# Attention probabilities turned in 32 x 32 blocks on VectorE and rearranged through DRAM

## The chip, the cores and the metric

The kernel runs on one core of a Trainium2 chip. The metric is the time of one execution on the device, in microseconds (us). The engines of the core run their own instruction streams in program order and wait for each other by semaphores: TensorE (PE in the profile, its weight loads are PEld), VectorE (DVE), ScalarE (ACT), GpSimd (POOL) and SyncE (SP, which issues transfers). ScalarE and GpSimd can issue transfers too.

## The reference

One pre-norm decoder layer in float32 on 4 sequences of 512 tokens with 512 channels: gated linear attention, cross attention to 256 context tokens with quantized probabilities, and a block of causal attention with a mixture of experts. The change lies in the causal attention: 16 heads of 128 channels in 4 groups that share keys and values, cut here to its core.

```python
def causal_attention(x1, h):                 # one sequence, S = 512
    q, k = rope(rmsnorm(h @ wq)), rope(rmsnorm(h @ wk))
    v = h @ wv
    q, k, v = heads(q, 16), heads(k, 4), heads(v, 4)     # 128 channels each
    for head in range(16):
        s = q[head] @ k[head // 4].T / sqrt(128)
        p = softmax(where(causal, s, -inf))              # (queries, keys)
        o[head] = p @ v[head // 4]
    return x1 + concat(o) @ wo
```

TensorE sums over the partitions of both its operands. The probabilities come out with queries on partitions, and `p @ v` sums over keys, so each block of 128 x 128 of `p` must be brought to keys on partitions first.

## The kernel before

The 2048 tokens are worked in 16 blocks of 128 (number `i`, with `c = i % 4` the place in its sequence). Block `i` sees `c + 1` blocks of keys. Its attention runs over four groups `g` of four heads; the four heads of one group in one block are called a set here, 64 sets in all.

For a set, `scores` multiplies on TensorE (line 1333), masks the diagonal and finds the maxima on VectorE (1335 to 1337), exponentiates on ScalarE (1339) into four tiles `e[0]` to `e[3]`, one a head with 128 queries on partitions, and divides by the sums on VectorE (1341, 1343). `values` then turns each 128 x 128 block on TensorE against the identity (1364), four heads into one PSUM tile, copies that tile to SBUF on ScalarE (1366, tile `eT`, three buffers) and multiplies the 512 columns by the values' weights (1360, 1370) into the PSUM tile `po`, which VectorE copies to `oT` (1372). `project` multiplies by the output weights (1380).

`attention` runs these one set apart: `scores` of set g + 1, then `project` of g - 1, then `values` of g. The tiles of `e` come in two lots of four (`xa`, and `og` with `x_in`), so one set is scored while the other is used.

The functions are Python generators. `weave` interleaves several streams of them: the attention of block `i` at virtual time `i`, the projections `qkv` of a later block, cross attention (`crossing`, with `norms`), `rest_of` and others. Each `yield` is one step; the dictionary `steps` (lines 152, 153) says how many steps a generator is thought to have, and so how its steps are spread; after a first run of a kind the count found takes its place. The order so made is the program order of every engine.

PSUM tiles of the name `pb` come from a pool of six buffers, for all streams. Weights are loaded in pieces of 512 KB by SP (`load_q`, line 1230, four buffers; `load_o`, line 1239, three), each issued behind the matmul that freed its buffer. SP also stores and reloads activations through DRAM (271, 274, 279, 355, 1197, 1401, 1425, 1434, 1436). In cross attention SP stores the quantized queries (271) and reads them back in four transfers (279) that wait for that store.

At the end of the stage `load_experts` loads the expert weights (1690 to 1694) while the last block's attention runs; then the experts follow (`turned`, `gate_up`, `down`).

Of the kernel before, what the change touches and what calls it, by code (L numbers as in the profile page):

```python
# [31 lines left out]
F32 = mybir.dt.float32  # L32
BF16 = mybir.dt.bfloat16
AF = mybir.ActivationFunctionType
ALU = mybir.AluOpType
# [4 lines left out]
P = 128  # L40
B, S, D = 4, 512, 512
NT = B * S // P
TB = S // P
KD = D // P
# [60 lines left out]
def decoder(ctx: ExitStack, tc: tile.TileContext, a: dict, out: bass.AP):  # L105
    nc = tc.nc
# [6 lines left out]
    ident = tab[:, C_ID, :]  # L113
# [36 lines left out]
            yield from g  # L150

    steps = {"first_o": 3, "cross": 37, "qkv": 12, "rest_of": 5, "route": 10, "enter": 8, "spares": 24, "load": 26}
    steps.update((f"attention{c}", n) for c, n in enumerate((37, 41, 53, 57)))

    def weave(*streams):

# [46 lines left out]
    dram = ctx.enter_context(tc.tile_pool(name="dram", bufs=1, space=DRAM))  # L203
# [6 lines left out]
    def transposed(src, pool, name, bufs=2):  # L210

        kind, eye = (F32, ident) if src.dtype == F32 else (BF16, ident_i)
        tp = p_b.tile([P, KD, P], kind, name="pb")
        for kd in range(KD):
            nc.tensor.transpose(tp[:, kd, :], src[:, kd * P : (kd + 1) * P], eye)
        t = pool.tile([P, KD, P], kind, name=name, bufs=bufs)
        nc.scalar.copy(t, tp)
        return t
# [23 lines left out]
    hTs, x2s, xis, fronts = {}, {}, {}, {}  # L242
# [135 lines left out]
    with ExitStack() as st:  # L378
# [18 lines left out]
        p_b = st.enter_context(tc.tile_pool(name="a_pb", bufs=4, space=PSUM))  # L397
# [674 lines left out]
        start = prologue(0)  # L1072
# [69 lines left out]
    with ExitStack() as st:  # L1142
        keep = st.enter_context(tc.tile_pool(name="b_keep", bufs=1, reuse_waits="tile"))
        small = st.enter_context(tc.tile_pool(name="b_small", bufs=4, reuse_waits="tile"))
        p_b = st.enter_context(tc.tile_pool(name="b_pb", bufs=6, space=PSUM, reuse_waits="tile"))
# [3 lines left out]
        wa = st.enter_context(tc.tile_pool(name="b_a", bufs=2, reuse_waits="tile"))  # L1149
        mid = st.enter_context(ExitStack())  # L1150
        wq_ = mid.enter_context(tc.tile_pool(name="b_q", bufs=2, reuse_waits="tile"))
# [39 lines left out]
        def norms(i):  # L1191


            x2 = x2s.pop(i)
            x3 = wq_.tile([P, D], F32, name="x3", bufs=1)
            yield from layernorm(x3.unsqueeze(1), x2.unsqueeze(1), small)
            nc.sync.dma_start(x3d[i], x3)
            h = wq_.tile([P, D], F32, name="h3", bufs=1)
            ss = small.tile([P, 1], F32, name="rms_s")
            nc.scalar.activation(h, x3, AF.Square, accum_out=ss)  # L1200
            yield
            r = small.tile([P, 1], F32, name="rms_r")
            rsqrt(r, ss, small, add=1e-6, mul=1.0 / D)
            yield
            nc.vector.tensor_scalar(h, x3, r, None, ALU.mult)
            yield
            tp = p_b.tile([P, KD, P], F32, name="pb")
            hTs[i] = wq_.tile([P, KD, P], F32, name="hT", bufs=2)
            for kd in range(KD):
                nc.tensor.transpose(tp[:, kd, :], h[:, kd * P : (kd + 1) * P], ident)  # L1210
            for kd in range(KD):
                nc.scalar.activation(hTs[i][:, kd, :], tp[:, kd, :], AF.Identity, scale=ln1[:, kd : kd + 1])
            yield
# [35 lines left out]
                load_o()  # L1249
                yield  # L1250

        zero = wa.tile([P, 4, P], F32, name="eT", bufs=3).rearrange("p a b -> p (a b)")
        nc.gpsimd.memset(zero, 0.0)
        nc.gpsimd.dma_start(hd[CAP : CAP + P], zero)
        nc.gpsimd.dma_start(spares[0 : 2 * NE * P].rearrange("(p n) c -> p (n c)", p=P), zero[:, 0 : 4 * NE])
# [60 lines left out]
        def scores(i, g, out):  # L1316

            c = i % TB
            at = (i - c) % RING
            runs = [(0, at, min(c + 1, RING - at))]  # L1320
            if at + c + 1 > RING:
                runs.append((RING - at, 0, at + c + 1 - RING))
            nk = (c + 1) * P
            qT, rq = qs[i]
            both = 2 if c < 2 else 1
            e = [ao.tile([P, S], F32, name="xa", bufs=4) for _ in range(4)] if g % 2 == 0 else [ao.tile([P, S], F32, name=n, bufs=2) for n in ("og", "og", "x_in", "x_in")]
            es = small.tile([P, 4], F32, name="es")
            nm = small.tile([P, 4], F32, name="nm")
            for n in range(0, 4, both):
                ps = p_b.tile([P, both, S // both], F32, name="pb")  # L1330
                for m in range(both):
                    for k, j, w in runs:
                        nc.tensor.matmul(ps[:, m, k * P : (k + w) * P], qT[g][:, n + m, :], kT[:, g, j : j + w, :], start=True, stop=True)  # L1333
                diag = ps[:, :, nk - P : nk]
                nc.vector.tensor_tensor(diag, diag, over(tab[:, C_CAUSAL, :], both), ALU.add)
                nc.vector.tensor_reduce(nm[:, n : n + both], ps[:, :, :nk], AX.X, ALU.max, negate=True)
                nc.vector.tensor_scalar(nm[:, n : n + both], nm[:, n : n + both], rq, None, ALU.mult)
                for m in range(both):
                    nc.scalar.activation(e[n + m][:, :nk], ps[:, m, :nk], AF.Exp, bias=nm[:, n + m : n + m + 1], scale=rq, accum_out=es[:, n + m : n + m + 1])  # L1339
                yield  # L1340
            nc.vector.reciprocal(es, es)
            for n in range(4):
                nc.vector.tensor_scalar(e[n][:, :nk], e[n][:, :nk], es[:, n : n + 1], None, ALU.mult)
            out.append(e)
            yield

        def attention(i):


            c = i % TB  # L1350
            vals = [kv[k] for k in range(i - c, i + 1)]
            oTs = []

            def values(g, e):
                po = p_1.tile([P, 4, P], F32, name="po")
                eTs = []
                for k in range(c + 2):
                    if k > c:
                        yield
                        nc.tensor.matmul(po, vals[c][:, g, :], eTs[c], start=c == 0, stop=True)  # L1360
                        break
                    tp = p_b.tile([P, 4, P], F32, name="pb")
                    for n in range(4):
                        nc.tensor.transpose(tp[:, n, :], e[n][:, k * P : (k + 1) * P], ident)  # L1364
                    eT = wa.tile([P, 4, P], F32, name="eT", bufs=3)
                    nc.scalar.copy(eT, tp)  # L1366
                    eTs.append(eT)
                    yield
                    if k:
                        nc.tensor.matmul(po, vals[k - 1][:, g, :], eTs[k - 1], start=k == 1, stop=False)  # L1370
                oTs.append(wa.tile([P, 4, P], F32, name="oT"))
                nc.vector.tensor_copy(oTs[-1], po)  # L1372
                yield

            def project(g):
                oT = oTs.pop(0)
                for h in range(0, 4, 2):
                    w = ahead_o.pop(0)
                    for m in range(2):
                        nc.tensor.matmul(pw, oT[:, h + m, :], w[:, m, :], start=g == 0 and h + m == 0, stop=g == 3 and h + m == 3)  # L1380
                    load_o()
                    yield

            es = early.pop(i, [])
            if not es:
                yield from scores(i, 0, es)
            for g in range(4):
                if g < 3:
                    yield from scores(i, g + 1, es)
                elif i + 1 < NT:  # L1390
                    while i + 1 not in qs:
                        yield
                    early[i + 1] = []
                    yield from scores(i + 1, 0, early[i + 1])
                if g == 1:
                    pw = p_1.tile([P, D], F32, name="pw")
                if g > 0:
                    yield from project(g - 1)
                if g == 3:
                    x3 = wa.tile([P, D], F32, name="x3_in")  # L1400
                    nc.sync.dma_start(x3, x3d[i])
                yield from values(g, es.pop(0))
            del qs[i]
            yield
            yield from project(3)
            nc.vector.tensor_tensor(x3, pw, x3, ALU.add)
            xs[i] = x3
# [13 lines left out]
        def rest_of(i):  # L1421

            x1 = xs.pop(i)
            x2 = ao.tile([P, D], F32, name="acc", bufs=1)
# [10 lines left out]
            nc.gpsimd.tensor_tensor(x2, x2, x1, ALU.add)  # L1435
            stored.append(nc.sync.dma_start(out[i * P : (i + 1) * P], x2).ins.name)
            yield
            hT = transposed(h, wa, "eT", bufs=3)
            yield

            parts = p_b.tile([P, P], F32, name="pb")
# [275 lines left out]
        for i in range(NT - 1):  # L1717
            g, kind = rest_of(i), "rest_of"
# [49 lines left out]
        def turned(b):  # L1768
            t = rows_of.pop(b)
            tp = p_b.tile([P, KD, P], F32, name="pb")  # L1770
            for kd in range(KD):
                nc.tensor.transpose(tp[:, kd, :], t[:, kd, :], ident)
            hTs[b] = wa.tile([P, KD, P], F32, name="eT", bufs=3)
            nc.vector.tensor_copy(hTs[b], tp)

        def gate_up(b):
# [128 lines left out]
```

## Time and profile before

| | |
|---|---|
| time, median of 3 runs | 3330.07 us (3327.7 to 3330.5) |
| the profiled execution's own time, and its span | 3329.88 us, 3328.1 us |
| attention stage (first score block to line 1406 of the last) | about 1951 to 3096 us |
| in it: PE, DVE, ACT, POOL busy | 1119, 706, 592, 228 us |
| transfers from 1950 to 3100 us | 216 MB, SP's hardware queue 56.7% of the 16 DMA engines' time |

The profile lists, for one execution, busy time by engine, groups of instructions by source line, and the order of time. Matmuls are pipelined, so the price of one is the distance between starts and not its listed duration; a float32 matmul is listed as two passes. A float32 transpose is one pass of 128 columns. Issues of transfers on SP and ScalarE are listed as SPq and ACTq and don't count as busy.

### The profile page before, as it was taken

The page shows a single profiled execution, that of the slowest core. Times are in us where ns is not written, and L with a number is a line of the kernel's source. Part 1 is how long each engine was busy: PE and PEld are TensorE (multiplying, and loading weights), DVE is VectorE, ACT ScalarE, POOL GpSimd, SP SyncE. Part 2 cuts the span into 40 slices and gives each one's busy share as a digit, 9 for nine tenths or more (in the row PEclk, how much of TensorE's full clock was granted, in tenths as well). Part 3 has the DMA queues.
Part 4 walks back from the last instruction along what each step waited for, and adds up shares of the span by engine and source line. Part 5 has one row for each costly group of instructions (what it writes and reads, how often), then busy time and mean ns, then how long its engine had stood idle before and what let it go on. Part 6 is the DMA issues. An engine that isn't in the chain of part 4 may idle for free. (4 is left out here: it accounts for less than half of the span.)

```text
span 3328.1 us, 48186 instructions
## 1 busy us (share of the span) xinstructions
PE 3166.4 (95%) x16015; PEld 1775.2 (53%) x16015; DVE 1831.9 (55%) x4184; ACT 1606.6 (48%) x4391; POOL 1465.7 (44%) x2780
## 2 busy tenths in 40 slices
PE   5899999999999999999998789999999999999998
PEld 3555555555555555555555445555555555555444
DVE  5665555546555556555454566656665665646211
ACT  3445555545554455545453346455555555645222
POOL 1156757676666666676765211112212221121443
PEclk8999999999999999999998799999999999999999
DMA  6343534444444434454434455556655565567454
GB/s 171 103 134 114 145 103 131 138 124 126 118 129 137 133 117 121 124 148 126 121 108 120 144 178 185 176 161 186 183 167 165 184 168 155 175 198 263 93 89 60
DMA packets 491032, 476.09 MB, mean 143 GB/s; under 512 B 225332, under 2 KB 340554, under 8 KB 490656
## 3 DMA queue, kind: packets, MB, share of 16 engines
q1 hardware_dynamic: 477616, 444.59, 45.5%
q0 software_dynamic: 11728, 25.58, 3.8%
q8 instruction: 128, 2.10, 0.3%
q10 hardware_dynamic: 1440, 2.84, 0.3%
q14 instruction: 120, 0.98, 0.1%
HBM read 411.23 MB, written 61.69 MB: 142 GB/s over the span
## 5 line engine op out<-in xcount | busy, mean ns | idle before, releaser
L598 PE MATMUL pb<-xnT,w 128*128 128x512 f32 x2048 | 958.6, 603 | 0.5 <-DVE at L674 0.2
L598 PEld LDWEIGHTS pb<-xnT,w 128*128 128x128 f32 x2048 | 364.8, 192 | 340.4 <-issue 333.5
L609 DVE SCALAR_TENSOR_TENSOR cv<-pb,pp,cv 128x510 f32<-128x510 f32 (+2 forms) x576 | 424.3, 746 | 92.7 <-ACT cv L606 79.4
L752 POOL TENSOR_TENSOR iT<-iT,iW 64x126 f32<-64x126 f32 (+22 forms) x930 | 344.7, 371 | 72.8
L1267 PE MATMUL pb<-c_q,hT 128*128 128x512 f32 x768 | 353.0, 599 | 3.3 <-DMA c_q<-in_c_wq_dram 1.6
L751 POOL TENSOR_TENSOR iW<-iA,iT 64x126 f32<-64x126 f32 (+22 forms) x930 | 321.6, 346 | 65.7 <-issue 0.2
L1186 POOL TENSOR_TENSOR rope_s<-q,tab 128x128 f32<-128x128 f32 x80 | 45.0, 563 | 481.6 <-DVE q L1297 368.3
L972 PE MATMUL pb<-wot,og 128*128 128x512 f32 x512 | 247.6, 607 | 5.5 <-DVE xa L977 4.5
L1267 PEld LDWEIGHTS pb<-c_q,hT 128*128 128x128 f32 x768 | 141.4, 192 | 157.4 <-issue 147.3
L606 ACT ACTIVATE cv<-pb,pp 128x512 f32<-128x512 f32 x192 | 148.7, 774 | 148.1 <-PE pb L598 144.2
L653 POOL TENSOR_TENSOR rk<-ss,mhalf 128x8 f32<-128x8 f32 x32 | 77.7, 2428 | 276.3 <-DVE ss L652 276.3
L977 DVE TENSOR_TENSOR xa<-pb,xa 128x512 f32<-128x512 f32 x112 | 77.1, 688 | 187.2 <-PE pb L972 187.2
L306 ACT ACTIVATE x_e<-pb,nm,x_step 128x256 f32<-128x256 f32 x256 | 141.2, 565 | 57.8 <-DVE nm L302 56.7
L1380 PE MATMUL pw<-wot,oT 128*128 128x512 f32 x344 | 162.6, 599 | 1.6 <-DVE oT L1372 1.3
L1333 PE MATMUL pb<-kT,qT 128*128 128x256 f32 (+3 forms) x576 | 163.2, 409 | 0.8 <-ACT og L1339 0.7
L705 POOL TENSOR_TENSOR qg<-qh,row 128x512 f32<-128x512 f32 x64 | 82.8, 1293 | 171.7 <-ACT qh L612 149.2
L972 PEld LDWEIGHTS pb<-wot,og 128*128 128x128 f32 x512 | 92.6, 192 | 100.2 <-issue 89.2
L612 ACT ACTIVATE qh<-cv 128x512 f32<-128x512 f32 x64 | 40.4, 631 | 212.8 <-DVE cv L609 212.8
L1782 PE MATMUL pb<-w_gu,eT 128*128 x288 | 130.3, 595 | 3.1 <-issue 3.1
L1366 ACT COPY eT<-pb 128x512 f32<-128x512 f32 x160 | 91.5, 596 | 85.2 <-PE pb L1364 84.3
L132 POOL TENSOR_TENSOR rms_r<-rsq,mhalf 128x1 f32<-128x1 f32 x48 | 27.3, 570 | 220.4 <-DVE rsq L131 220.4
L458 ACT ACTIVATE em<-em,ee 128x128 f32<-128x128 f32 x256 | 78.3, 388 | 94.5 <-POOL ee L655 81.6
(436 smaller groups left out, 6239.9 us busy)
## 6 DMA issues: line engine op xcount, KB each, us to landing
c_q<-in_c_wq_dram SPq DMA_DIRECT2D x128, 512.0 KB
w<-in_a_w_dram SPq DMA_DIRECT2D x124, 512.0 KB
wot<-in_c_wo_dram SPq DMA_DIRECT2D x86, 512.0 KB
row<-g_d SPq DMA_DIRECT2D x64, 512.0 KB
c_o<-in_c_wo_dram SPq DMA_DIRECT2D x42, 512.0 KB
at_d<-at SPq DMA_DIRECT2D x64, 256.0 KB
rrow<-r_d SPq DMA_DIRECT2D x32, 512.0 KB
T<-t_d SPq DMA_DIRECT2D x32, 512.0 KB
```

The source lines that it names most:

```text
L306: nc.scalar.activation(e[:, 2 * r + g, :], ps[r][:, g, :], AF.Exp, bias=nm[:, r, g : g + 1], scale=step[:, h : h + 1], accum_out=ssum[:, g ...
L598: nc.tensor.matmul(pj, wt[:, kd, p * P : (p + 1) * P], xnT[:, kd, :], start=kd == 0, stop=kd == KD - 1)
L606: nc.scalar.activation(ac, pj, AF.Identity, bias=cb[:, m, h : h + 1], scale=cw[:, m, h, 3:4])
L609: nc.vector.scalar_tensor_tensor(ac[:, j:], pj[:, : S - j], cw[:, m, h, 3 - j : 4 - j], ac[:, j:], ALU.mult, ALU.add)
L751: eng.tensor_tensor(u, A[:, i, i + 1 :].unsqueeze(2).to_broadcast([nb, n, w]), T[:, i, :w].unsqueeze(1).to_broadcast([nb, n, w]), ALU.mult)
L752: eng.tensor_tensor(T[:, i + 1 :, :w], T[:, i + 1 :, :w], u, ALU.add)
L972: nc.tensor.matmul(pw, og[p][:, c * P : (c + 1) * P], wot[:, p, :], start=p == 0, stop=p == HG - 1)
L1267: nc.tensor.matmul(pj, hT[:, kd, :], w[:, kd % 2, :], start=kd == 0, stop=kd == KD - 1)
L1333: nc.tensor.matmul(ps[:, m, k * P : (k + w) * P], qT[g][:, n + m, :], kT[:, g, j : j + w, :], start=True, stop=True)
L1366: nc.scalar.copy(eT, tp)
L1380: nc.tensor.matmul(pw, oT[:, h + m, :], w[:, m, :], start=g == 0 and h + m == 0, stop=g == 3 and h + m == 3)
L1782: nc.tensor.matmul(pg, hT[:, kd, :], w_gu[:, bass.ds(e, 1), kd, :, :], start=kd == 0, stop=kd == KD - 1)
```

## The change

The transposes on TensorE, their PSUM tiles and the copies on ScalarE go. In their place, at the end of `scores`:

1. VectorE turns each head's probabilities in blocks of 32 x 32 (four instructions a set, 128 x 128(c + 1) each), into one tile `t` with one buffer. Within each quarter q of 32 partitions, keys now lie where queries lay: partition q*32 + j holds, for block b of 32 keys in key block k, head n and query i, the probability of query q*32 + i and key k*128 + b*32 + j.
2. SP writes each quarter to DRAM, with rows by key (four transfers a set, 64 to 256 KB each).
3. After two empty steps ScalarE issues four transfers that read them back, keys on partitions, into the four tiles of `e`. Tile `e[q]` now holds the queries of quarter q of all four heads.

`values` multiplies for each quarter 128 columns, for each block of keys, with the values' weights loaded again for each. The output comes out by quarters, and the copy to `oT` puts it into order by heads; it moves from VectorE to ScalarE. The counts in `steps` are raised. Since `t` takes space, other tiles share or lose theirs: `h3` goes (its values are written over `x2`, its squares into `hT`), `x3_in` has one buffer in place of two, and tiles that used `eT` go to `hT` and `oT`.

```diff
-    steps.update((f"attention{c}", n) for c, n in enumerate((37, 41, 53, 57)))
+    steps.update((f"attention{c}", n) for c, n in enumerate((89, 79, 85, 83)))
...
-            h = wq_.tile([P, D], F32, name="h3", bufs=1)
+            hTs[i] = wq_.tile([P, KD, P], F32, name="hT", bufs=2)
             ss = small.tile([P, 1], F32, name="rms_s")
-            nc.scalar.activation(h, x3, AF.Square, accum_out=ss)
+            nc.scalar.activation(hTs[i].rearrange("p k t -> p (k t)"), x3, AF.Square, accum_out=ss)
...
-            nc.vector.tensor_scalar(h, x3, r, None, ALU.mult)
+            nc.vector.tensor_scalar(x2, x3, r, None, ALU.mult)
...
             for n in range(4):
                 nc.vector.tensor_scalar(e[n][:, :nk], e[n][:, :nk], es[:, n : n + 1], None, ALU.mult)
+            yield
+
+            t = wa.tile([P, 4 * S], F32, name="eT", bufs=1)[:, : 4 * nk].rearrange("p (b k n i) -> p b k n i", b=4, n=4, i=32)
+            for n in range(4):
+                nc.vector.transpose(t[:, :, :, n, :].rearrange("p b k i -> p k b i"), e[n][:, :nk].rearrange("p (k b j) -> p k b j", b=4, j=32))
+                if n % 2:
+                    yield
+
+            d = dram.tile([4, P, S], F32, name="p_d", bufs=3)
+            for q in range(4):
+                nc.sync.dma_start(d[q].rearrange("(b j) x -> j b x", b=4)[:, :, :nk], t[q * 32 : (q + 1) * 32].rearrange("p b k n i -> p b (k n i)"))
+                if q % 2:
+                    yield
+            yield
+            yield
+            for q in range(4):
+                nc.scalar.dma_start(e[q][:, :nk], d[q][:, :nk])
+                if q % 2:
+                    yield
             out.append(e)
             yield
...
             def values(g, e):
                 po = p_1.tile([P, 4, P], F32, name="po")
-                eTs = []
-                for k in range(c + 2):
-                    if k > c:
-                        yield
-                        nc.tensor.matmul(po, vals[c][:, g, :], eTs[c], start=c == 0, stop=True)
-                        break
-                    tp = p_b.tile([P, 4, P], F32, name="pb")
-                    for n in range(4):
-                        nc.tensor.transpose(tp[:, n, :], e[n][:, k * P : (k + 1) * P], ident)
-                    eT = wa.tile([P, 4, P], F32, name="eT", bufs=3)
-                    nc.scalar.copy(eT, tp)
-                    eTs.append(eT)
+                for q in range(4):
+                    for k, val in enumerate(vals):
+                        nc.tensor.matmul(po[:, q, :], val[:, g, :], e[q][:, k * P : (k + 1) * P], start=k == 0, stop=k == c)
                     yield
-                    if k:
-                        nc.tensor.matmul(po, vals[k - 1][:, g, :], eTs[k - 1], start=k == 1, stop=False)
                 oTs.append(wa.tile([P, 4, P], F32, name="oT"))
-                nc.vector.tensor_copy(oTs[-1], po)
+                nc.scalar.copy(oTs[-1].rearrange("p n (q i) -> p q n i", q=4), po.rearrange("p q (n i) -> p q n i", n=4))
                 yield
...
-                    x3 = wa.tile([P, D], F32, name="x3_in")
+                    x3 = wa.tile([P, D], F32, name="x3_in", bufs=1)
...
-            hT = transposed(h, wa, "eT", bufs=3)
+            hT = transposed(h, wa, "hT", bufs=1)
...
-            hTs[b] = wa.tile([P, KD, P], F32, name="eT", bufs=3)
+            hTs[b] = wa.tile([P, KD, P], F32, name=("oT", "oT", "hT")[b % 3], bufs=(2, 2, 1)[b % 3])
```

More of the change, by code (lines that the diff above doesn't have):

```diff
@@ L1204, in norms @@
             yield
-            nc.vector.tensor_scalar(h, x3, r, None, ALU.mult)
+            nc.vector.tensor_scalar(x2, x3, r, None, ALU.mult)
             yield
             tp = p_b.tile([P, KD, P], F32, name="pb")
-            hTs[i] = wq_.tile([P, KD, P], F32, name="hT", bufs=2)
             for kd in range(KD):
-                nc.tensor.transpose(tp[:, kd, :], h[:, kd * P : (kd + 1) * P], ident)
+                nc.tensor.transpose(tp[:, kd, :], x2[:, kd * P : (kd + 1) * P], ident)
             for kd in range(KD):
@@ L1250, in first_o @@
                 yield
-        zero = wa.tile([P, 4, P], F32, name="eT", bufs=3).rearrange("p a b -> p (a b)")
+        zero = wa.tile([P, 4 * S], F32, name="eT", bufs=1)[:, 0:S]
         nc.gpsimd.memset(zero, 0.0)
```

## The prediction

> **What bounds the kernel now.** I read the page's busy shares first, then a table of busy time by stretch, one stretch for each block of 128 queries in the attention stage (cut where line 1406 ends a block), then the order of time of TensorE, and last the order of time and the waits of SP's queue. From the page and the table:
>
> ```profile
> PE 3166.4 (95%) x16015; PEld 1775.2 (53%) x16015; DVE 1831.9 (55%) x4184; ACT 1606.6 (48%) x4391; POOL 1465.7 (44%) x2780
> ...
> 2025.00:2101.00 76.00, 73.80 (x330) 39.47 (x329) 47.61 (x127) 38.65 (x107) 13.82 (x21) 1.00 0.55 175
> 2175.00:2257.00 82.00, 81.90 (x345) 42.93 (x344) 49.91 (x133) 43.44 (x113) 11.60 (x19) 1.00 0.50 157
> 2257.00:2327.00 70.00, 66.40 (x320) 36.34 (x319) 47.66 (x167) 38.68 (x108) 14.17 (x22) 1.00 0.67 201
> 3048.00:3096.00 48.00, 47.70 (x183) 24.48 (x182) 27.11 (x90) 22.21 (x45) 10.94 (x11) 1.00 0.86 279
> ```
>
> Columns: stretch, its length, busy us of PE, PEld, DVE, ACT, POOL, then granted clock, DMA share, GB/s. The stage runs from 1951 to 3096. TensorE is busy 1119 of these 1145 us at full clock; VectorE has 706, ScalarE 592. So TensorE bounds the stage, and what is taken from it comes back in full, as long as no other engine makes it wait. The last stretch differs: only the sixteenth block is left in it, and its DMA share is 0.86, since the expert weights are being loaded.
>
> **What TensorE saves.** From the order of time of TensorE (start, us, line, shape, count):
>
> ```profile
> 2032.00 0.60 PE L1364 MATMUL pb<-tab,xa 128*128 128x128 f32 x4
> 2032.44 3.60 PE L1267 MATMUL pb<-c_q,hT 128*128 128x512 f32 x8
> 2035.88 3.60 PE L259 MATMUL pb<-wq,xT 128*128 128x512 f32 x8
> ...
> 2261.35 0.66 PE L1333 MATMUL pb<-kT,qT 128*128 128x128 f32 x4
> 2261.85 0.38 PE L338 MATMUL pb<-tab,x_by 128*128 128x128 f32 x2
> ```
>
> Starts tell the price, since matmuls overlap. Four transposes take 2032.44 - 2032.00 = 0.44 us. Eight passes over 512 columns take 3.44, so 0.43 each; a float32 matmul is two passes, 0.86. Passes of 128 columns with other weights each time (line 1333) run at 0.50 / 4, at most 0.125; the transposes' 0.11 is the lower bound, and 512 columns / 4 says 0.108. For one set and one block of keys the old way costs 0.44 + 0.86 = 1.30. The new one costs four matmuls of 128 columns, eight passes, 0.86 to 1.00; I take 0.89 (0.111 a pass, near the long run). Four blocks of tokens of each c, four sets each, c + 1 blocks of keys: 160 such pieces. Saved: 160 x 0.41 = **65 us** (48 at 0.125). Of it 11 to 12 us lie in the last two blocks.
>
> **What VectorE and ScalarE get.** VectorE loses 64 copies of line 1372 (0.685 each, 44 us) and gets 256 turns of 128 x 128(c+1). No such operation is in the trace; the nearest rows are the scaling of line 1343, which goes from SBUF to SBUF (0.42 us a piece at 512 columns by its starts), and the PSUM copy of line 1372 (0.685). I take 0.60 at 512 and 0.36 at 128: 16 x (1.44 + 1.76 + 2.1 + 2.4) = 123 us. VectorE then stands at 706 - 44 + 123 = 785 of some 1100: not a bound.
>
> ScalarE loses 160 copies of line 1366 (0.596 each, 95 us), gets the 64 output copies with their columns reordered (same PSUM source and size, so 0.6 to 0.69: 40 us) and issues 256 transfers:
>
> ```profile
> L1366 ACT COPY eT<-pb 128x512 f32<-128x512 f32 x160 | 91.5, 596 | 85.2 <-PE pb L1364 84.3
> ...
> 1.65 0.45 ACTq L405 DMA_DIRECT2D pp<-in_a_chan_dram  x1
> ...
> 6.32 7.77 ACTq L589 DMA_DIRECT2D w<-in_a_w_dram  x4
> ```
>
> The only issues on ScalarE lie at the start: 0.45 when its queue is free, 1.9 each where it is backed up. I take 0.45: 115 us. ScalarE works 592 - 95 + 40 + 115 = 652 us. By work alone it would be no bound either.
>
> **The added wait.** Each read is issued by ScalarE and needs its write to have landed. Until then everything behind it in ScalarE's program stands still: exponentials of both attentions, squares, PSUM copies. How long? The chain from a set's last scores on, in one set with c = 3:
>
> ```profile
> 2503.70 1.03 PE L1333 MATMUL pb<-kT,qT 128*128 128x256 f32 x4
> ...
> 2506.97 0.80 ACT L1339 ACTIVATE xa<-pb,nm,rq 128x512 f32<-128x512 f32 x1
> 2508.32 1.67 DVE L1343 TENSOR_SCALAR xa<-xa,es 128x512 f32<-128x512 f32 x4
> ```
>
> From the exponential's end (2507.77) to the scaled probabilities (2509.99) are 2.2 us. Then four turns (2.4), four issues on SP (0.35 each, 1.4), and the landing of the last write. For that SP's queue gives rows:
>
> ```profile
> 2514.73 0.34 SPq L271 DMA_DIRECT2D x_q_d<-x_qi  x1
> 2518.18 7.56 SPq L279 DMA_DIRECT2D x_qT<-x_q_d  x4
> ...
> 2630.29 0.36 SPq L1436 DMA_DIRECT2D out_dram<-acc  x1
> 2634.35 0.34 SPq L1425 DMA_DIRECT2D acc<-x2d  x1
> ...
> SPq L1425 <- DMA out_dram<-acc: 55.8, 14, 7.4
> SPq L279 <- DMA x_q_d<-x_qi: 25.9, 11, 4.8
> ```
>
> The second of each pair waits for the first's landing in DRAM: 3.45 us after issue for 128 KB, 4.06 for 256 KB. The waits (sum, times, longest) run from 25.9 / 11 = 2.4 on average at one line to 7.4 at worst at the other: these are my two ends. I take 4.0 for c = 3 and 3.4 for c = 0. So the last read is issued 2.2 + 2.4 + 1.4 + 4.0 + 0.45 = 10.5 us after the last exponential, and about 7.9 where c = 0. The eight steps between them, of some 83 in a block, hold ScalarE's work for other streams: 43.4 - 16 exponentials at 0.87 - 9.5 of copies = 20 us a block, so 1.9. ScalarE is out of service for 8.6 us a set at c = 3 and 6.0 at c = 0, 7.3 on average, in a set of 15 to 20 us.
>
> **What covers it.** The data itself has time: a set is used one whole set after it was scaled (its first transposes started mostly 13 to 20 us after the scaling ended, by both lines' rows), and reads need some 4 us more. TensorE feels the pause through PSUM. It has six `pb` tiles, almost all emptied by ScalarE. Without the transposes a block takes 47 (scores 12 on average, projections and their transposes 11, cross attention 20, the rest 4), one each 1.5 us: six last 9.2. Off go 1.5 for making and reading a tile and 1.5 that ScalarE already lags (2504.7 to 2506, above): 6.2 us of cover. So 2.4 us are missing at c = 3 and none at c = 0, 1.1 on average. Add 0.4 for sets whose writes queue on SP behind the four slow issues of line 279 (7.56 us of a 76 us block, half of it on average: 0.1 x 3.8). **1.5 us a set**, times 56 sets of the first fourteen blocks: 84 us. The ends: with landings of 2.4 the pause fits the cover, 0; with 7.4 it is 3.4 us longer, nearly 4 a set once the lag is carried on, 224. SP is held too, since a write waits there for the turns: behind it stand weight loads (lines 1230, 1239), which have some 10 us of lead; I count them at 0 and put their failure with the third case below.
>
> **The last block** has no other work to hide in. From the last scores to values lie now, for TensorE, two projections of 3.4, one set's values of 3.5 and one set's scores of 3.4: 13.7 us. The chain needs 1.2 + 0.9 + 2.2 to the scaling, 2.4 of turns, and two landings under a DMA share of 0.86, at 7.4 for the write and 6 for the read: 21 with issues. Two sets are under way, so a stall of 21 - 13.7 = 7.3 falls on every second one, and the last, with no scores behind it (10.3 of cover, and the 7.3 just lost), stalls 3.4: **18 us**. With landings of 4.0 it is 1.9 twice and 3.4: 7.
>
> **Sum.** The profiled execution took 3329.9 us (span 3328.1), within 0.2 us of the median of the runs, 3330.1. 3329.9 - 65 + 84 + 18 = **3367**.
>
> **Two rules.** The Trainium skill, in "VectorE: DVE Perf Modes", section "Rules for kernel authors", speaks against the change: a 128 x 128 transpose belongs on TensorE where PSUM may take it, since VectorE turns only within 32 x 32 blocks. The section on the three paths gives 311 ns for one 128 x 128 in bf16 on VectorE; no trace here shows it. As an estimate by that figure, ten blocks a set (on average) with 3.1 us instead of 1.9 would lengthen each pause by 1.2 us and the sum, by 67, to about 3434. "DMA: Bandwidth & Descriptors", section "Anatomy of one DMA", holds a fixed 2 us and the bytes at 436 GB/s, about 2.6 us for 256 KB, where the rows above show 4.06. By it each pause is about 1.4 us shorter, the stall some 0.7 a set, that of the last block 10, and the sum about 3314.
>
> **The cases.** (1) The pause outruns the cover as above: 3367, between 3340 and 3430. Chance 0.45. (2) Faster: the pause fits, since ScalarE is paused just when no score tiles are due, and half its time is free to catch up. Only the last block stalls: 3329.9 - 65 + 7 to 18, **3278**. For it speaks the lead of the data; against it that ScalarE's 652 us of work and 64 x 7.3 = 467 of pause come to 1119, more than TensorE's 1065. Chance 0.33. (3) Much slower: SP holds loads back. Each set holds SP from the write's place to the end of the turns, and 80 MB of new packets raise the DMA share from 0.57 (210 MB over 1150 us) to about 0.79. If loads miss their lead by 2 us in each of the 56 sets: +112, **3480**. It decides from the point where a weight load lands over 10 us after its buffer came free. Against it: TensorE waits now for c_q only 1.6 us in total. Chance 0.15. The remaining 0.07 is a balance within 0.2% (6.7 us, about what runs of this kernel can tell from no change).
>
> The range from 3275 to 3480 leaves the outer parts of (2) and (3) out; the likeliest case's own is 3340 to 3430. Faster 0.33, same 0.07, slower 0.60.
>
> **What would show it.** Right: lines 1364 and 1366 gone, TensorE's busy time in the stage lower by about 65, idle time of ScalarE ended by DMA at the reads (several us a set), and TensorE's idle time ended by ScalarE grown to about 100 us. Wrong: ScalarE's waits for the writes under 2 us a set, turns over 1 us at 512 columns, or TensorE waiting for c_q or wot.

## The result and the profile after

The changed kernel takes 3421.5 us (median of 4 runs, 3411.8 to 3426.7), the one before 3329.2 (4 runs, 3327.7 to 3330.5): 1.0274 times as long, interval 1.025 to 1.0297. The profiled execution took 3411.8 us (span 3409.9); span against span it is 81.8 us longer. The forecast of 3367 had the direction, but put the loss at 37 us instead of 92 (82 in the profiled execution).

The page's busy times of the after kernel:

```profile
PE 3148.1 (92%) x16335; PEld 1823.7 (53%) x16335; DVE 1887.8 (55%) x4376; ACT 1555.4 (46%) x4295; POOL 1466.1 (43%) x2780
```

TensorE has less to do than before (3166.4) and is idle more. The whole difference lies in the attention stage. Its table by stretch (the first fourteen blocks, then the last two; columns as in the prediction), first of the kernel before:

```profile
1945.00:2995.00 1050.00, 1024.91 (x4453) 555.86 (x4452) 649.47 (x1852) 547.12 (x1485) 209.28 (x308) 0.99 0.57 175
2995.00:3096.00 101.00, 100.49 (x368) 51.84 (x367) 57.21 (x177) 46.41 (x103) 18.55 (x21) 1.00 0.73 238
```

then of the kernel after:

```profile
1942.00:3037.00 1095.00, 1007.38 (x4752) 593.30 (x4751) 701.53 (x2046) 511.78 (x1420) 213.17 (x308) 0.97 0.76 233
3037.00:3179.00 142.00, 99.11 (x385) 62.61 (x385) 59.47 (x175) 31.77 (x72) 18.71 (x21) 0.83 0.80 259
```

Length less PE busy is idle time: 25 and 0.5 us before, 88 and 43 after. The last column but two is the granted clock: 0.97 and 0.83 after. Half of the busy time in the stretches at half clock is lost; added up from the trace's clock records and TensorE's busy time, this comes to 4.0 us before and 43.1 after. So the stage closes as a sum of three:

| us, attention stage | before | after | difference |
|---|---|---|---|
| TensorE's work, at full clock | 1121.0 | 1063.5 | -57.5 |
| TensorE idle | 25.6 | 130.5 | +104.9 |
| lost at half clock | 4.0 | 43.1 | +39.1 |
| stage | 1150.6 | 1237.1 | +86.5 |

Outside the stage the after kernel is 4.7 us shorter. The half clock is seen in the order of time of TensorE, by equal groups:

```profile
2166.16 1.88 PE L1387 MATMUL pw<-wot,oT 128*128 128x512 f32 x4
...
2171.76 1.56 PE L1376 MATMUL po<-og,val 128*128 128x128 f32 x12
...
3079.52 0.94 PE L1376 MATMUL po<-og,val 128*128 128x128 f32 x6 [1.67 <-DMA og<-p_d]
3083.55 3.38 PE L1376 MATMUL po<-x_in,val 128*128 128x128 f32 x12 [3.09 <-DMA x_in<-p_d]
3087.66 3.78 PE L1387 MATMUL pw<-wot,oT 128*128 128x512 f32 x4 [0.73 <-ACT oT L1379]
```

After waits of 1.67 and 3.09 us for reads, four matmuls of line 1387 take 3.78 us instead of 1.88, and twelve of line 1376 take 3.38 instead of 1.56. A table cut to that stretch gives the clock as 0.50:

```profile
3083.00:3096.00 13.00, 10.65 (x32) 7.38 (x32) 4.25 (x9) 3.10 (x7) 0.00 (x0) 0.50 0.80 268
```

Where TensorE idles is told by its waits (sum, times, longest), after:

```profile
PE po L1376 <- DMA xa<-p_d: 39.9, 23, 8.5
PE po L1376 <- DMA og<-p_d: 23.4, 8, 5.8
...
PE po L1376 <- DMA x_in<-p_d: 9.0, 3, 5.7
```

At these three rows the product with the values waits until the reads have landed: 72 of the 130 us. Idle time ended by ScalarE came to 28 us (11 before), where the forecast put about 100. For weights (`c_q`, `wot`) TensorE waited 4.9 us, against 1.6 before. What made the reads late starts with where ScalarE issues them. Its order of time around the reads of the fourth block's first set (c = 3):

```profile
2171.51 0.60 ACT L1295 ACTIVATE q<-pb 128x512 f32<-128x512 f32 x1 [2.54 <-PE pb L1266]
...
2173.62 0.33 ACTq L1359 DMA_DIRECT2D xa<-p_d  x1
2177.52 0.60 ACT L1295 ACTIVATE q<-pb 128x512 f32<-128x512 f32 x1 [4.42 <-DMA xa<-p_d]
...
2178.96 0.33 ACTq L1359 DMA_DIRECT2D xa<-p_d  x1
...
2182.95 0.81 ACTq L1359 DMA_DIRECT2D xa<-p_d  x2
```

The four reads of one set do not go out together behind one wait: they are spread over 10 us, with other streams' work between them. ScalarE's idle time just before reads adds up to 86 us, 1.3 a set and not 7.3, but the last read goes out late: on average over the twelve sets of blocks 4, 8 and 12 (c = 3) its issue ends 23.1 us after the set's last exponential, where the forecast had 10.5 (turns ended at 6.6, writes issued by 12.1 and landed at 16.0). It lands at 27.9.

The second place is SP. Its waits before weight loads and writes, before:

```profile
SPq L1230 <- PE pb L1267: 312.5, 127, 12.1
...
SPq L1239 <- PE pw L1380: 211.0, 76, 13.3
```

and after:

```profile
SPq L1229 <- PE pb L1266: 97.1, 45, 11.6
SPq L1238 <- PE pw L1387: 88.0, 29, 8.3
SPq L1353 <- DVE eT L1347: 66.1, 25, 7.8
SPq L1238 <- DMA xa<-p_d: 65.6, 23, 6.4
...
SPq L1229 <- DMA xa<-p_d: 44.9, 12, 7.8
...
SPq L1229 <- DMA og<-p_d: 28.8, 11, 5.7
...
SPq L1229 <- DMA p_d<-eT: 22.9, 18, 4.7
...
SPq L1238 <- DMA og<-p_d: 21.6, 5, 8.3
```

Before, SP waited at a load for TensorE to free its buffer, so it was early. After, it stands 194 us before loads (the five rows at lines 1229 and 1238 that name `xa`, `og` or `p_d`, and 9.7 at line 1238 for writes) for reads and writes whose data the loads do not touch. By the semaphores' numbers, all transfers of SP and ScalarE report their landing at the same eight, in turn, and nearly every one waits until the one eight places before it has landed. So the reads of ScalarE hold the loads of SP. What this stand cost is a question for the experiments: TensorE waited for weights only the 4.9 us named above.

### The profile page after: what moved, and what is told of

The parts are those of the page before. It is cut to its first block, busy times and chain, and to the rows that moved or that the text cites. A ratio compares the mean times of both kernels' runs of the same rounds, so it can differ in the third digit from the quotient of the medians.

```text
span 3409.9 us, 49776 instructions
## 1 busy us (share of the span) xinstructions
PE 3148.1 (92%) x16335; PEld 1823.7 (53%) x16335; DVE 1887.8 (55%) x4376; ACT 1555.4 (46%) x4295; POOL 1466.1 (43%) x2780
## 5 line engine op out<-in xcount | busy, mean ns | idle before, releaser
L1376 PE MATMUL po<-xa,val 128*128 128x128 f32 x640 | 97.8, 299 | 40.0 <-DMA xa<-p_d 39.9
L1376 PEld LDWEIGHTS po<-xa,val 128*128 128x128 f32 x640 | 88.2, 207 | 64.1 <-DMA xa<-p_d 34.8
```

The source lines that it names most:

```text
L1376: nc.tensor.matmul(po[:, q, :], val[:, g, :], e[q][:, k * P : (k + 1) * P], start=k == 0, stop=k == c)
```

## The experiments

The theories named in the expectations are these. A: the forecast's, ScalarE's pause before the reads. B: late data, TensorE stands at the values. C: the weight loads on SP are held back by the new transfers, by their count through the eight landing semaphores ("marks"). D: their bytes. S puts C more widely: a queue that works in order stands at each write until the turns are done and at a mark until it is free. K is the half clock. Times are of one execution each, beside one of before (3325.8 to 3333.9); the after kernel's four span 15 us, so smaller differences are not weighed. Differences to the after kernel are taken from its profiled execution, 3411.8, the fastest of the four; from their median each gain would be 10 us larger.

**No transfers (e1).** The eight transfers are replaced by empty steps and the values use `e` as it is; this leaves out bringing the blocks to their keys.

> Leaves out all eight transfers of a set; TensorE multiplies the values with the scaled probabilities as they stand on their queries. Everything else of the change stays: the turns on VectorE, the 128-column matmuls, the output copy on ScalarE, the empty steps, the smaller buffers. Theory A (ScalarE's pause for the writes), B (the reads land after TensorE wants them) and C (the reads hold SP's queue, since SP's own transfers wait for marks that the reads give back) all say that the whole loss is in the transfers: 3260 to 3290 us. If turns, copies or smaller buffers cost something themselves, it stays above 3310.

Measured 3270.7: 59 us faster than before, as far as the saving of TensorE reaches. By stretch:

```profile
1946.00:2946.00 1000.00, 968.90 (x4719) 572.22 (x4718) 692.48 (x2024) 504.10 (x1409) 212.17 (x308) 0.99 0.59 184
2946.00:3038.00 92.00, 87.63 (x423) 54.41 (x421) 65.47 (x196) 36.05 (x83) 18.69 (x21) 1.00 0.80 265
```

The turns (VectorE 692, as after) cost nothing visible. All 141 us up to 3411.8 come with the transfers.

**Which wait? (e2, e3, e4.)** One wait is taken away each time.

```diff
# e2: values read a constant table; transfers and their waits stay;
# leaves the probabilities out of the output
-  nc.tensor.matmul(po[:, q, :], val[:, g, :], e[q][:, k * P : (k + 1) * P], ...)
+  nc.tensor.matmul(po[:, q, :], val[:, g, :], tab[:, C_ROPE + k, :], ...)
# e3: reads fetch weight rows and wait for no write;
# leaves the probabilities out of the output
-  nc.scalar.dma_start(e[q][:, :nk], d[q][:, :nk])
+  nc.scalar.dma_start(e[q][:, :nk], a["c_wo"][q * P : (q + 1) * P, :nk])
# e4: reads issued by GpSimd
-  nc.scalar.dma_start(e[q][:, :nk], d[q][:, :nk])
+  nc.gpsimd.dma_start(e[q][:, :nk], d[q][:, :nk])
```

> Transfers, waits and traffic stay as in the changed kernel, but the matmuls of the values read a constant table in place of the probabilities that came back, so TensorE never waits for the reads. B: the stalls at the values go, 3270 to 3300 us. A: the pause of ScalarE is still there, 3370 to 3420. C: SP's queue is still held, loads still late, 3350 or more.

> The reads fetch rows of an input (output weights) of the same size, so ScalarE needn't wait for the writes to land; the writes go to DRAM as before and nobody reads them. A: the pause is gone, 3280 to 3300 us. B: the way from the turns to the data is shorter by the writes' landing, some 5 to 9 us a set, which is most of the lateness in the first fourteen blocks and half of it in the last two: 3310 to 3340. C: the reads go out earlier, so SP is held less: about 3310.

> The four reads of a set are issued by GpSimd in place of ScalarE, with the same wait for the writes. ScalarE has no pause at all, and SP's transfers share no marks with the reads. A: 3290 to 3310 us. B: the data comes as late as before, 3390 to 3430. C: SP's loads are free of the reads, so writes go out in time: 3330 to 3370.

Measured 3394.3, 3383.0 and 3436.2. With the values free (e2) TensorE's idle time did not fall (130.1 us); its waits only changed their name:

```profile
PE pw L1387 <- DMA wot<-in_c_wo_dram: 39.6, 2, 39.1
PE pw L1387 <- DMA c_o<-in_c_wo_dram: 17.2, 3, 9.3
PE pb L1266 <- DMA c_q<-in_c_wq_dram: 10.8, 2, 6.9
```

So weights are late behind the late data, 68 us in these rows, but 53 of them lie in the last two blocks, 39.1 in a single wait. In the first fourteen blocks most was ended by ScalarE (39 of 74 us). B alone is not it; nor does the wait for the writes give more than 29 us (e3). e4 leaves ScalarE nothing to issue or to wait for, and is no faster, with 8 us of TensorE's idle time ended by ScalarE: A falls as the main cause. C's 3330 to 3370 for e4 was missed as well: its loads stand less than 1 us for new transfers, against 194, and nothing came back.

**Count or bytes? (e9, e10, e11.)** e9 joins e2 and e3, so no transfer waits for a write and TensorE waits for none. e10 moves 32 columns in each of the same eight. e11 is the whole computation with the four writes as one (`t` of 128 partitions to `d`, rows of all quarters side by side) and reads from `d[:, q * 32 : (q + 1) * 32, :nk]`.

> All eight transfers of each set stay, with their bytes, but the values product reads a constant table and the reads fetch rows of a weight in DRAM, so that nothing waits for a write to land and TensorE waits for no read. It leaves out the probabilities in the output. Theory B (late data: TensorE stands at the values until the reads land, or the reads stand until the writes have landed) has nothing left to lose: 3265 to 3290, near the 3270.7 of the kernel without transfers. Theory C (count: every transfer of SP and ScalarE takes one of eight landing marks in turn, so the weight loads on SP wait for earlier transfers of either queue) and theory D (bytes: some 84 MB more traffic makes each load slower) both say that the weight loads still come late: 3330 to 3380.

> The same as the one without waits, but each of the eight transfers of a set moves only 32 columns instead of 128 to 512: the count of transfers and their order stay, a tenth of the bytes is left (32 of 320 columns on average). Theory D (bytes): 3265 to 3290, the loss is gone with the bytes. Theory C (count and order of the landing marks): within 15 us of the kernel without waits, which it puts at 3330 to 3380. Theory B gives 3265 to 3290 for both.

> The whole computation. The four writes of a set become one transfer of 128 partitions, and the four reads stay: five transfers a set instead of eight, 192 fewer issues on SP. Theory C (count): three eighths of what the marks hold back come back, and SP is 1 us a set less busy: 3360 to 3395. Theory B (late data): one transfer lands at about the same time as the last of four, so 3400 to 3420. Theory D (bytes): unchanged, 3400 to 3420.

Measured 3385.2, 3373.2 and 3661.4. e9 has no late data, and keeps 114 of the 141 us; nine tenths fewer bytes give 12 back, no more than executions of one kernel differ by. So on these two queues it is mainly count and order that cost, not bytes. In e9 TensorE stands for weights:

```profile
PE pw L1387 <- DMA wot<-in_c_wo_dram: 30.9, 4, 24.7
PE pb L1266 <- DMA c_q<-in_c_wq_dram: 26.6, 9, 6.0
PE pw L1387 <- DMA c_o<-in_c_wo_dram: 16.5, 2, 13.1
```

In e10 that falls from 74 to 25 us, but idle time ended by VectorE (45) and ScalarE (35) takes its place. SP's waits in e9:

```profile
SPq L1353 <- DVE eT L1347: 82.6, 22, 10.8
...
SPq L1353 <- DMA c_q<-in_c_wq_dram: 43.4, 24, 4.3
...
SPq L1353 <- DMA xa<-in_c_wo_dram: 42.4, 21, 7.8
...
SPq L1353 <- DMA og<-in_c_wo_dram: 29.0, 16, 4.7
```

It stands for the turns, and for marks. A reservation: freed of the writes, the reads go out right behind the turns, and ScalarE stood some 88 us for those. e11 missed every theory, since it changed more than the count: at c = 3 its write lands 8.1 us after issue (median; 5.0 for the four) and its reads 11.8 (5.0). Their source now has an outermost dimension of four. The Trainium skill, "DMA: Bandwidth & Descriptors", section "Rules for kernel authors", says that a transfer whose outermost dimension is below 16 stays on at most that many engines. The trace agrees: each of these reads updates its landing semaphore 5 times, almost all of the after kernel's 16 times; no run changes this alone. e11 tells nothing of the count.

**The last two blocks (e5).** For `i >= 14` the old `values` runs, with TensorE's transposes.

> The last two blocks of 128 queries (the fifteenth and sixteenth) turn their probabilities on TensorE as before, the other fourteen as after. If the last two blocks lose by themselves, because no work of other blocks is left to hide two landings behind: their 142 us fall to 100 to 108, and the whole to 3365 to 3380. If they only pay for what earlier blocks left late (loads that are behind, a throttled clock): 120 us or more for the two, 3390 or more in all.

Measured 3394.9. The two blocks do fall from 142 to 104 us, at full clock:

```profile
3050.50:3154.50 104.00, 103.50 (x374) 53.11 (x373) 57.50 (x178) 45.81 (x104) 15.24 (x19) 1.00 0.71 244
```

They lose 38 us by themselves, as the first branch said; but 10 came back in the first fourteen blocks (1105.5 us) and 8 behind the stage, so 17 are left of it, and the branch's 3365 to 3380 was missed. Every kernel here that turns the last blocks in the old way (e5, e22, e23, e25) takes 238 to 239 us behind the stage, the one before 232 and the one after 230, so these 8 us go with the old way at the end; why stays open.

**Later reads (e7).** Six empty steps instead of two between writes and reads.

> The whole computation; six steps of other work instead of two lie between the writes and the reads, and the counts of steps are raised by as much. Theory A (ScalarE stands at the reads until the writes have landed, 1.5 us a set beyond its cover): four more steps shorten each stand by about 1 us, 3350 to 3390. Theory B (the reads come too late for TensorE): they come later still, 3425 to 3460. Theory S: within 10 us of 3411.8, since the writes keep their place on SP.

Measured 3416.1: within the after kernel's own four times. It speaks against A, and B's loss did not come either; S's "within 10 us" held.

**Other queues (e15, e16, e17, e20), and the writes alone (e19, e24).** e15 issues all eight on GpSimd, e17 only the writes; e16 is e9 with all eight on GpSimd; e20 is e16 with 32 columns. e19 keeps only the writes; e24 is e19 with six empty steps ahead of them. All but e15 and e17 leave the probabilities, or their order, out of the output.

> The whole computation; all eight transfers of a set are issued by GpSimd instead of SP and ScalarE, with the same waits. So the weight loads on SP stand behind no write and share no landing mark with the new transfers, and ScalarE issues nothing. Theory S (a queue that works in order stands still at a write until the turns are done and at a transfer until its landing mark is free, and the weight loads behind it are late): 3310 to 3350, as far as GpSimd's own work has slack. Theory B (late data): writes and reads land no earlier than after, 3390 to 3420. If GpSimd, standing at the waits, becomes the late one (its rotations and powers feed VectorE and TensorE): over 3420, as with the reads alone on GpSimd.

> All eight transfers issued by GpSimd, and the values product reads a constant table and the reads fetch weight rows, so that nothing waits for a write to land and TensorE waits for no read. It leaves out the probabilities in the output. Theory S (standing queues of SP and ScalarE): 3275 to 3310, since both queues are as they were without transfers and only GpSimd waits for the turns. Theory D (bytes on the DMA engines): as with these transfers on SP and ScalarE, 3370 to 3390.

> The whole computation; the writes are issued by GpSimd, the reads by ScalarE as in the after kernel: the fourth of the two by two of queues (3411.8 after, 3436.2 with the reads on GpSimd, 3396.0 with both). Theory S: SP stands at no write, 3375 to 3400. If the reads' stand on ScalarE and the shared landing marks are what holds SP: 3400 to 3420. Theory K: lost at half clock between 0.25 and 0.45 of the idle time over 25 us.

> As with all eight transfers on GpSimd and no waits (3361.9), but each transfer moves 32 columns: the count and the places on GpSimd stay, a tenth of the bytes is left. It leaves out the probabilities in the output. Theory D in a weaker form (on GpSimd nothing holds SP, and what is left is the longer landing of the weight loads, 9.2 us instead of 6.8 at the ninetieth percentile): 3270 to 3300. Theory S for GpSimd (its own work stands behind the writes): within 15 us of 3361.9.

> The four writes of a set stay on SP, the reads are gone, and the values product takes the scaled probabilities as they are. It leaves out the reads, and so the order of the probabilities in the output. Theory S says how much of the 141 us over the kernel without transfers the writes' place on SP costs by itself: about half, 3320 to 3350. Theory A (ScalarE's pause for the reads) and theory B (late reads): 3270 to 3285, since nothing waits for a read.

> The kernel with the writes alone (3337.25), with six more steps of other work between the turns and the writes. It leaves out the reads, and so the order of the probabilities in the output. Theory S (SP comes to the write before the turns are done, 203 us in all, and the weight loads behind it are late): with the writes later in SP's order that stand shrinks, 3280 to 3310. If the bytes of the writes are what costs: 3327 to 3345. Theory K (every us that TensorE idles costs about a third of a us more at half clock): the time lost at half clock stays between 0.25 and 0.45 of the idle time over 25 us.

| writes, reads on | us | who stands |
|---|---|---|
| SP, ScalarE (after) | 3411.8 | SP before loads 194 us, before writes 154; ScalarE before reads 86 |
| SP, GpSimd (e4) | 3436.2 | SP before writes 227, GpSimd before reads, for the writes, 115 |
| GpSimd, ScalarE (e17) | 3427.5 | ScalarE before reads 203 |
| GpSimd, GpSimd (e15) | 3396.0 | GpSimd before both, below |
| GpSimd, no waits (e16) | 3361.9 | GpSimd for the turns, 236 |
| the same, few bytes (e20) | 3317.2 | GpSimd for the turns, 348 |
| SP, no reads (e19); later (e24) | 3337.3; 3325.7 | SP before writes 220; 154 |

e15 frees SP and ScalarE, but missed S's 3310 to 3350: the stand turns up on GpSimd, whose rotations of queries and keys feed TensorE:

```profile
POOL p_d L1353 <- DVE eT L1347: 179.8, 44, 11.9
...
POOL xa L1359 <- DMA p_d<-eT: 68.9, 37, 4.8
...
POOL og L1359 <- DMA p_d<-eT: 58.7, 19, 8.0
```

e17 missed S's 3375 to 3400 and lies above the other branch's 3420: with SP free, ScalarE's pause, which the forecast had feared, appears at 203 / 64 = 3.2 us a set. S is right that something stands, not that one queue is to blame. In e4, e15 and e17 the loads stand at most 6 us for new transfers, 194 after, and the best of the three gives 16 us; that the stand at shared marks costs time of its own is not shown. The writes alone cost 3337.3 - 3270.7 = 67 us, as S had it; moved later they cost 55, so S's 3280 to 3310 was missed, and most of that price is not SP's stand at the turns. In both, TensorE waits for weights (47 and 44 us) and the loads of line 1229 land in 8.1 us at the ninetieth percentile against 6.8 in e1, so the writes' bytes are a rival there; no run takes the bytes alone out of e19. Bytes matter where no queue of the loads stands: e16 to e20 gives 45 us (13 of them behind the stage), and these loads land in 9.2 us against 6.9. Both missed every range put for them. Even e20, which waits for no landing and moves little, gains only 9 us on the kernel before, measured with it (3325.8), and that is too little to weigh.

**Only the richest sets (e22, e23).** Old `values` everywhere except blocks 4, 8 and 12 (c = 3), on SP and ScalarE, and on GpSimd.

> The whole computation; only the sets of blocks 4, 8 and 12 (four blocks of keys, where a set saves TensorE most: 1.64 us for the same eight transfers) go the new way, all others turn on TensorE as before. Saving 12 x 1.64 = 20 us. If a set costs what it costs on average, 141 / 64 = 2.2 us, the sum is 3329.9 - 20 + 26 = 3336. If twelve sets among old ones find cover (in the after kernel two of the three blocks with four blocks of keys were 6 us shorter than before): 3310 to 3325. If the coupling of queues costs more than that in each: 3340 or more.

> The same three blocks, with all eight transfers issued by GpSimd. All on GpSimd was 15 us faster than on SP and ScalarE over 64 sets, so 3 us for twelve: 3307 to 3322 if the twelve sets find cover, 3333 if each costs the average.

Measured 3347.8 and 3359.0, beside 3325.8. Some 6 to 7 us of that lie behind the stage and come with the old way at the end, as above. In the stage, idle time and the half clock grew by 32 and 41 us over before's 30: 2.7 and 3.4 us for each of the twelve sets, beside the 2.2 of the average. So a set's round trip found no cover where its neighbours leave the queues alone, and neither kernel came into the range put for that case; e22's third branch, 3340 or more, held. **Both helpful edits together (e25)**, all on GpSimd and the last two blocks old:

> The whole computation; all eight transfers on GpSimd and the last two blocks turned on TensorE as before: the two edits that helped, together. If they add up: 3396.0 - 17 = 3379, and in any case between 3365 and 3390, slower than before.

Measured 3381.0: they add up, and it is slower than before. No version that does the whole computation beat the kernel before.

**The half clock (K)** in TensorE's ledger of the stage, work at full clock being 1047 to 1068 where all sets go the new way:

| us | before | e1 | e20 | e24 | e19 | e16 | e10 | e15 | e7 | e2 | after | e17 | e4 | e11 |
|---|---|---|---|---|---|---|---|---|---|---|---|---|---|---|
| idle | 26 | 35 | 66 | 74 | 84 | 93 | 105 | 121 | 123 | 130 | 130 | 134 | 146 | 305 |
| lost at half clock | 4 | 5 | 19 | 19 | 20 | 21 | 37 | 37 | 51 | 30 | 43 | 50 | 53 | 110 |

Over before's 26 and 4 us, lost time is 0.25 to 0.48 of the idle time, 0.37 after, in every kernel but e1, where little idles. (e7 lies just over K's 0.45, e17 at 0.43, e24 at 0.31.) No kernel held the idle time and kept the clock, so that the stalls cause it is read from the traces, not shown by an edit; the last section has the reading that ties each halving to the idle time just ahead of it.

## Why the prediction missed

- **Bound and saving.** TensorE does bound the stage. Saved were 57.5 us of work at full clock, not 65 (69.6 in e1, without the transfers; where those 12 went stays open).
- **The step that failed** is the price of stalls: "1.5 us a set" from ScalarE's pause, 84 us, and 18 for the last block, with nothing for the clock. Of the 130 us of idle time in the stage, 72 were waits for reads at the values and 28 were ended by ScalarE, and the half clock took 43 us, 39 more than before. Idle time grew by 104.9, near the 102 of these two terms, and that is a coincidence of size. In the first fourteen blocks it grew by 63 instead of 84 and in the last two by 42 instead of 18, and the place was another: late reads at the values and, where these are taken away (e2, e9), late weights. That the measured 3421.5 lies within case (1)'s own 3340 to 3430 is luck too: two of the signs that the forecast named against itself came, ScalarE's waits under 2 us a set and TensorE waiting for weights (4.9 us after, 74 in e9).
- **The clock** was left out, though one of the sixteen stretches read for the forecast showed what idle time does to it, 6.5 us idle and a clock of 0.96:

```profile
2625.00:2705.00 80.00, 73.51 (x312) 39.63 (x311) 47.94 (x125) 38.23 (x106) 21.84 (x30) 0.96 0.60 175
```

  It cost 39 us. With it, the forecast's own terms would have come to 3406, beside 3411.8 in the profiled execution; as the idle term agreed by coincidence, so does this sum.
- **The chain of a set** was too short: 10.5 us to the last read's issue were 23.1. Turns ended 2 us late, the writes stood on SP (issued by 12.1 instead of 6.0), the last landed 4.0 us after its issue ended, as put, and the reads were spread over 8. "The data itself has time" was said with some 4 us for reads; it had not.
- **ScalarE's pause**, 7.3 us a set, was 1.3: the reads were put where their writes had mostly landed. The eight steps between, of some 83 in a block of 76 us, are about 7 us by the forecast's own figures, and it took off only ScalarE's work in them, 1.9. The pause is larger where the writes leave SP (3.2 in e17). PSUM's cover was hardly tried: TensorE's idle time ended by ScalarE, where its lack would show, grew from 11 to 28.
- **SP "at 0"** was not safe. The writes stood 154 us on SP, and the writes alone cost 67 us (e19). Loads stood 194 us behind the new transfers, mostly at shared semaphores, which the forecast did not see; but TensorE waited only 4.9 us for weights in the after kernel, so case (3) did not come as it was told, and the cost of this stand is not shown. DMA share rose to 0.76, as put (0.79); bytes were a small part while SP and ScalarE carried them (12 us).
- **Durations** held: turns 0.265 to 0.712 us listed, VectorE 761 us in the stage (785 put), ScalarE's issues 0.33 (0.45 put). The rule that the Trainium skill has against the change ("VectorE: DVE Perf Modes", section "Rules for kernel authors") was right: not the turns cost (e1), but the way that blocks turned within 32 x 32 still have to go to their keys. Its "DMA: Bandwidth & Descriptors", section "Anatomy of one DMA", with 2 us and the bytes at 436 GB/s, given there for transfers that GpSimd issues, was short of what SP and ScalarE took: 256 KB landed in 5.0 us (median, write and read). TensorE's time in case (2) should read 1119 - 65 = 1054, not 1065; nothing rests on it.

What stays open is how the 105 us of idle time split among the waits: they stand in for each other, so taking out one gives at most 30 us, and such gains do not add up to the 141. Shown is that 95 of them come with the transfers: without these, TensorE idles 35 us (e1).

## What to carry to other kernels

Before a block is sent through DRAM, follow the whole trip of one set (produce, issue, land, issue, land, use) and all that its queues carry besides; e1's kind of kernel, with the transfers left out, prices it in one run: its gain over the kernel before, here 59 us or 0.9 a set, is all that the trip may cost. A wait put on a queue that works in order is not removed by moving it to another queue; look who is behind it there. Where TensorE is the bound, a stall can cost more than its length: here the half clock added a quarter to a half of the idle time, so look for it in the profile.

## What the hardware showed that was not expected

- The granted clock has two values in these records, 1.0 and 0.5, and the halved stretches are multiples of 3.4 us (3.4 to 13.7). The Trainium skill, "TensorE: Matmul & The Clock Gate", section "HAM oscillation — how this bites in real kernels", warns of idle gaps of more than about 3.4 us. Here no single gap of that length is needed. In the attention stage of each of the 20 kernels the halved stretches begin on a grid of 3.413 us, and they go by TensorE's idle time in the step of the grid just ahead: of the steps at full clock with under 1.4 us idle none was followed by a halving (5,563), of those with more than 2.0 us all were (239), in between 32 of 174. In the after kernel 1.8 us made of gaps of 0.68 and 1.33 us were enough.
- A transfer on ScalarE can hold back a load on SP that shares no data with it, through the landing semaphores: loads stood 194 us for new transfers in the after kernel, none in e15. What that costs is not shown.
- VectorE turns 128 x 512 in float32 in 0.67 us and 128 x 128 in 0.27 (medians); the row for half of the turns, with all four shapes (shortest, median, longest in ns):

```profile
L1347 DVE STREAM_TRANSPOSE eT<-xa x128: 265/488/712, 1955.4 to 3129.5; 128x128 f32<-128x128 f32 x32, 128x256 f32<-128x256 f32 x32, 128x384 f32<-128x384 f32 x32, 128x512 f32<-128x512 f32 x32
```
